# A two-layer transformer block with modulated norms: the last feed-forward, batch by batch, inside the last slots of the attention before it

## Chip, cores and metric

One core of a Trainium2 chip runs the whole program. The time is device microseconds of one execution; the profile is of one such execution. Engines are named as in the profile: PE (TensorE, with PEld for its weight loads), DVE (VectorE), ACT (ScalarE), POOL (GpSimd) and SP (SyncE, here only a queue of transfers). All data are float32 in memory.

## What is computed

Two layers on x of 2 batches, 512 rows and 512 columns. Each is a modulated norm, an attention with a gate, another modulated norm and a feed-forward with a gate. The change concerns the end of layer 1:

```python
h = _layernorm(x) * (1 + ca) + sa
x = x + ga * _L1_attn_ref(h, ...)        # 128 heads, latent 64, head size 4, softmax over 512 keys
h = _layernorm(x) * (1 + cb) + sb
x = x + gb * _L1_ffn_ref(h, ...)

def _L1_ffn_ref(x, base_W, base_b, router_W, router_b, A, B, expert_map):
    base_out = einsum('btd,od->bto', x, base_W) + base_b
    probs = softmax(x @ router_W.T + router_b)          # 15 router outputs
    topk_p, topk_i = top_k(probs, 8)
    w = sum of topk_p over the chosen outputs that expert_map sends to each of 8 experts
    h = einsum('btd,erd->bter', x, A)                   # rank 16 for each expert
    return base_out + einsum('bter,eor->bto', h * w[..., None], B) * 2
```

## The kernel before

Tokens are 8 tiles of 128 rows (`xs[t]`, four for each batch); `hT[b]` holds a batch's normed input turned, features on partitions.

**Layer 1's attention** (`attention1`, from L732) goes over 64 quads: 8 groups of 16 heads (`g`), for each 2 batches, for each 4 quads of 4 heads. For a quad and each of 4 key blocks `i` and two pairs of heads `p`: PE makes scores (`rope`, L948 and L957), ACT copies them out (`keep`, L967), DVE keeps a running maximum (`largest`, L974), transposes it in blocks (`blocks`, L979) and reduces it (`tops`, L985). `twice`, `join` (a PE transposition, `psx`, L997), `top`, `top_hi`, `top_lo`, `stripes` and `row` spread a row's maximum over the keys. It is subtracted on DVE for a quad's first head (`less_even`, L1050) and on POOL for the three others (L1048 and L1054), for two of them from copies that ACT makes (`row_copy`, L1039) and for the third from `row_even` (L1043). ACT takes the exponential (L1057), PE mixes with the values (`mix`, L1103).

The order on the four engines is written out: `PLAN1` (L713 to L729) names for each slot the operations and, by a number, the quad they serve, so that a quad is spread over several slots (`tops 1 -2` is that step for the quad two slots back). `tc.manual_schedule` keeps this order. After a batch's last quad, `leave` (L1111) copies the sum out and puts pieces into two lists: `chain` (`inverse`, `back` and `exact`, `spreading`, `scale` and `both`) and, every second group, `later` (four times `project`, `gated`, `added`), which `extra`, `extra_dve` and `extra_pool` take up in later slots. The loop runs four slots past the last quad, and then empties the lists: the drain. SP's transfers aren't part of the order written out by hand; a scheduler places them.

**The feed-forward** (L393 to L492) has pools of its own and is ordered by the scheduler. Transfers of all its weights and constants come first, the small ones on POOL's queue (L411 to L417). Then for both batches the norm (`Norm.batch`, L205: statistics, root, rows `xn` L184, 16 PE transpositions L193, copies to `hT` with gain and shift, L201 on DVE and L203 on ACT), and on POOL the bias added to x (L428). Then for each batch: 16 router matmuls of 15 columns (`pl`, L434) and 4 that add the router's bias (L441); softmax; for each tile, a rank of every output by five DVE instructions on 15x15 comparisons (L457 to L462: greater, equal, equal times `before`, their sum, a reduction); `psel`, its four transpositions, a matmul to expert weights (`pw`, L472), the low-rank input (`ph`, L475), their product `hw`; and for each tile four matmuls with W (L485), one with the low-rank output (L488), the gate on DVE (L490), x added on POOL (L491) and the output's transfer.

Of the kernel before, what the change touches and what calls it, by code (L numbers as in the profile page):

```python
# [10 lines left out]
F32 = mybir.dt.float32  # L11
# [31 lines left out]
def adaln_kernel(ctx: ExitStack, tc: tile.TileContext, A: dict, out: bass.AP):  # L43
# [19 lines left out]
    ones_row = const.tile([1, P], F32, tag="ones_row", name="ones_row")  # L63
    nc.gpsimd.memset(ones_row, 1.0)
# [81 lines left out]

    def gated_bias(name, gate, pool):

        row = pool.tile([P, D], F32, tag="biasrow", name=f"row_{name}")
        nc.sync.dma_start(out=row, in_=A[name].unsqueeze(0).to_broadcast([P, D]))  # L150
        out = [pool.tile([P, D], F32, tag=f"gb{b}", name=f"gb{b}_{name}") for b in range(B)]
        for b in range(B):
            nc.gpsimd.tensor_mul(out[b], row, gate[b])
        return out
# [134 lines left out]


    with ExitStack() as c01:
# [99 lines left out]
        attention1(tc, A, small, hT, xs, gate[2], ident, normalised, c01.close)  # L391

    with ExitStack() as c3:  # L393
        lnp = c3.enter_context(tc.tile_pool(name="ln", bufs=1))
        fw = c3.enter_context(tc.tile_pool(name="ffn1", bufs=1))
        tmp = c3.enter_context(tc.tile_pool(name="tmp1", bufs=3))
        pmm = c3.enter_context(tc.tile_pool(name="pmm2", bufs=4, space=PSUM))
        gate[5] = gate_tiles(1, 5, fw)
        spread_gates(1, (2, 5), grow[1], pmm, {5: gate[5]})

        wT = fw.tile([P, KC, D], F32, tag="wT", name="wT1")
        nc.sync.dma_start(out=wT, in_=A["L1_ffn_WT"].rearrange("(kc p) o -> p kc o", p=P))
        rT = fw.tile([P, KC, N1], F32, tag="rT", name="rT1")
        nc.sync.dma_start(out=rT, in_=A["L1_ffn_RT"].rearrange("(kc p) n -> p kc n", p=P))
        aT = fw.tile([P, KC, E1 * R], F32, tag="aT", name="aT1")
        nc.sync.dma_start(out=aT, in_=A["L1_ffn_AT"].rearrange("(kc p) e -> p kc e", p=P))
        bT = fw.tile([P, D], F32, tag="bT", name="bT1")
        nc.sync.dma_start(out=bT, in_=A["L1_ffn_BT"])
        gb = gated_bias("L1_ffn_base_b", gate[5], fw)
        rb = fw.tile([1, N1], F32, tag="rb", name="rb1")  # L410
        nc.gpsimd.dma_start(out=rb, in_=A["L1_ffn_router_b"].unsqueeze(0))  # L411
        before = fw.tile([P, N1, N1], F32, tag="before", name="before")
        nc.gpsimd.dma_start(out=before, in_=A["c_before"])
        erow = fw.tile([N1, E1 * R], F32, tag="erow", name="erow")
        nc.gpsimd.dma_start(out=erow, in_=A["c_expert"])
        em_i = fw.tile([N1, 1], I32, tag="em_i", name="em_i")
        nc.gpsimd.dma_start(out=em_i, in_=A["L1_ffn_expert_map"].unsqueeze(1))  # L417
        em = fw.tile([N1, 1], F32, tag="em", name="em")
        nc.vector.tensor_copy(em, em_i)

        route = fw.tile([N1, E1 * R], F32, tag="route", name="route")
        nc.vector.tensor_scalar(route, erow, em, None, ALU.is_equal)

        norm = Norm(1, 3, 4, lnp)
        for b in range(B):
            norm.batch(b, pmm)
            for i in range(TB):
                nc.gpsimd.tensor_add(xs[b * TB + i], xs[b * TB + i], gb[b])  # L428
        for b in range(B):

            pl = pmm.tile([P, TB, N1], F32, tag="mm", name=f"pl{b}")
            for i in range(TB):
                for kc in range(KC):
                    nc.tensor.matmul(  # L434
                        pl[:, i, :],
                        lhsT=hT[b][:, kc, i * P : (i + 1) * P],
                        rhs=rT[:, kc, :],
                        start=(kc == 0),
                        stop=False,
                    )  # L440
                nc.tensor.matmul(pl[:, i, :], lhsT=ones_row, rhs=rb, start=False, stop=True)  # L441
            nm = small.tile([P, TB], F32, tag="nm", name=f"rnm{b}")
            nc.vector.tensor_reduce(nm, pl, AX.X, ALU.max, negate=True)
            pr = tmp.tile([P, TB, N1], F32, tag="pr", name=f"pr{b}")
            nc.vector.tensor_add(pr, pl, nm[:, :].unsqueeze(2).to_broadcast([P, TB, N1]))
            nc.scalar.activation(pr, pr, AF.Exp)
            rs = small.tile([P, TB], F32, tag="rs", name=f"rrs{b}")
            nc.vector.tensor_reduce(rs, pr, AX.X, ALU.add)
            nc.vector.reciprocal(rs, rs)
            nc.vector.tensor_mul(pr, pr, rs[:, :].unsqueeze(2).to_broadcast([P, TB, N1]))  # L450

            rank = tmp.tile([P, TB, N1], F32, tag="rank", name=f"rank{b}")
            for i in range(TB):
                pm = pr[:, i, :].unsqueeze(1).to_broadcast([P, N1, N1])
                pn = pr[:, i, :].unsqueeze(2).to_broadcast([P, N1, N1])
                gt = tmp.tile([P, N1, N1], F32, tag="gt", name=f"gt{b}_{i}")
                nc.vector.tensor_tensor(gt, pm, pn, ALU.is_gt)  # L457
                eq = tmp.tile([P, N1, N1], F32, tag="eq", name=f"eq{b}_{i}")
                nc.vector.tensor_tensor(eq, pm, pn, ALU.is_equal)
                nc.vector.tensor_mul(eq, eq, before)  # L460
                nc.vector.tensor_add(gt, gt, eq)
                nc.vector.tensor_reduce(rank[:, i, :], gt, AX.X, ALU.add)  # L462
            psel = tmp.tile([P, TB, N1], F32, tag="psel", name=f"psel{b}")
            nc.vector.scalar_tensor_tensor(psel, rank, E1 - 0.5, pr, ALU.is_lt, ALU.mult)
            pt = pmm.tile([P, 512], F32, tag="mm", name=f"pselT_ps{b}")
            for i in range(TB):
                nc.tensor.transpose(pt[:N1, i * P : (i + 1) * P], psel[:, i, :], ident)
            pselT = tmp.tile([N1, S], F32, tag="pselT", name=f"pselT{b}")
            nc.scalar.copy(pselT, pt[:N1, :])

            pw = pmm.tile([P, 512], F32, tag="mm", name=f"pw{b}")
            nc.tensor.matmul(pw, lhsT=route, rhs=pselT, start=True, stop=True)  # L472
            ph = pmm.tile([P, 512], F32, tag="mm", name=f"ph{b}")
            for kc in range(KC):
                nc.tensor.matmul(  # L475
                    ph, lhsT=aT[:, kc, :], rhs=hT[b][:, kc, :], start=(kc == 0), stop=(kc == KC - 1)
                )
            hw = tmp.tile([P, S], F32, tag="hw", name=f"hw{b}")
            nc.scalar.mul(hw, ph, 2.0)
            nc.vector.tensor_mul(hw, hw, pw)  # L480
            for i in range(TB):
                t, cols = b * TB + i, bass.ts(i, P)
                ps = pmm.tile([P, 512], F32, tag="mm", name=f"psf1_{t}")
                for kc in range(KC):
                    nc.tensor.matmul(  # L485
                        ps, lhsT=hT[b][:, kc, cols], rhs=wT[:, kc, :], start=(kc == 0), stop=False
                    )
                nc.tensor.matmul(ps, lhsT=hw[:, cols], rhs=bT, start=False, stop=True)  # L488
                y = tmp.tile([P, D], F32, tag="y", name=f"yf1_{t}")
                nc.vector.tensor_mul(y, ps, gate[5][b])  # L490
                nc.gpsimd.tensor_add(y, xs[t], y)  # L491
                nc.sync.dma_start(out=x_out[t * P : (t + 1) * P, :], in_=y)  # L492
# [239 lines left out]
def attention1(tc, A, small, hT, xs, ga, ident, normalised, close):  # L732
# [17 lines left out]
    with ExitStack() as ctx:  # L750
# [109 lines left out]
        chain, later = [], []  # L860
# [250 lines left out]
        def leave(t):  # L1111
# [52 lines left out]
            def gated(i, ps):  # L1164
                y = ap.tile([P, D], F32, tag="y", name=f"y1_{G}_{b}_{i}", bufs=2)
                nc.vector.tensor_mul(y, ps, ga[b])
                return y

            def added(i, y):
                nc.gpsimd.tensor_add(xs[b * TB + i], xs[b * TB + i], y)  # L1170

            chain.append((none, inverse, none))
            chain.append((none, back, exact))
            chain.append((spreading, scale, both if ty else none))
            chain.append(None)
            if ty:
                for i in range(TB):
# [47 lines left out]
        for w in range(2):  # L1225
            spread_up(0, w)
        with tc.manual_schedule(engines=FOUR):
            for t in range(-ahead[0] - 2, NQ - ahead[1]):
                n = t + ahead[0] + 1
                if 0 < n < NQ:  # L1230
                    wqs[n] = load_q(n)
# [5 lines left out]
                for d, f, args in plan:  # L1237
                    if f in ASIDE.values():
                        f(t, *args)
                    elif 0 <= t + d + (2 if f in early else 0) < NQ:  # L1240
                        f(t + d, *args)
# [92 lines left out]
```

## Time and profile before

| | us |
|---|---|
| median of 3 runs | 2544.6 (2543.75 to 2546.12) |
| the profiled execution | 2545.36 |
| its span in the profile | 2543.6 |
| quad 60's transposition `psx` on PE | 2333.2 |
| quad 61's, 62's, 63's | 2354.7, 2374.3, 2397.3 |
| end of the last quad's last `mix` | 2421.6 |
| end of the last projection of the attention | 2435.9 |
| last copies to `hT` of batch 1 end | 2453.0 |
| first `psf` matmul of batch 0, of batch 1 | 2480.6, 2521.1 |
| end of the last addition on POOL | 2540.5 |

Busy in the whole span: PE 2454.6 us, DVE 1672.9, ACT 1400.6, POOL 1592.2. Times in views are from the span's start. A line of the timeline or the chain gives start, duration, engine, line of the kernel and what it writes; "x8" stands for eight instructions that follow each other. A float32 matmul counts as two instructions. "Issue" in the chain is time in which the engine waited for nothing that the profile shows.

### The profile page before, as it was taken

Reading aid. Unit: us, or ns where it says so; the run is one execution under the profiler, and the core shown is the slowest. Engines: PE = TensorE matmul, PEld = TensorE weight load, DVE = VectorE, ACT = ScalarE, POOL = GpSimd, SP = SyncE. Lnnn points to the kernel's source line nnn. Section 1 sums busy time; section 2 is a strip of 40 time slices with the busy share of each in tenths; the row PEclk is TensorE's granted clock in tenths of the full one; section 3 lists DMA queues with packets and bytes.
Section 4 is the critical chain, followed back from the end, with each engine's and each line's share of the span. In section 5 each row is a group of like instructions: output and inputs, shape, how many; then the busy total and the mean of one; then the engine's idle time right before and its main releaser. Section 6 shows DMA issues by size and latency. Waiting matters only on the chain.

```text
span 2543.6 us, 28531 instructions
## 1 busy us (share of the span) xinstructions
PE 2454.6 (97%) x10268; PEld 1148.9 (45%) x10268; DVE 1672.9 (66%) x2323; ACT 1400.6 (55%) x2083; POOL 1592.2 (63%) x1538
## 2 busy tenths in 40 slices
PE   7999999999999999999999999999999999999757
PEld 3555555555555444444444344444444434444233
DVE  4545555555555345788777778777878777887652
ACT  2112212212112215888888788878888878888710
POOL 1333333333333314888888888888888888888841
PEclk9999999999999999999999999999999999999868
DMA  6211101001000101000000000000000000000010
GB/s 233 85 51 64 42 5 38 26 20 38 17 1 7 29 15 33 26 19 24 26 26 26 30 19 25 26 26 26 30 18 26 26 26 25 24 23 17 1 32 33
DMA packets 68477, 81.31 MB, mean 32 GB/s; under 512 B 6865, under 2 KB 49520, under 8 KB 68208
## 3 DMA queue, kind: packets, MB, share of 16 engines
q1 hardware_dynamic: 67984, 79.21, 9.8%
q8 instruction: 81, 1.33, 0.2%
q14 instruction: 60, 0.49, 0.1%
q0 software_dynamic: 352, 0.28, 0.1%
HBM read 77.38 MB, written 2.10 MB: 31 GB/s over the span
## 4 chain that ended last, share of the span: by engine, by line
PE 93%; issue 2%; DVE 2%; POOL 2%; ACT 1%; DMA 0%; SPq 0%; POOLq 0%; DVEq 0%; ACTq 0%
PE s L948 18%; PE psq L881 18%; PE acc L1103 9%; PE ps_q L552 9%; PE pw L664 8%; PE s L957 5%; PE s L603 4%; PE po L650 4%; PE psv L574 2%; PE ps_k L552 2%; PE pt L639 2%; PE psu L900 2%; PE psm L1027 1%; PE psw L1159 1%; PE psf L275 1%
## 5 line engine op out<-in xcount | busy, mean ns | idle before, releaser
L1054 POOL TENSOR_TENSOR ss<-ss,row 128x512 f32<-128x512 f32 x512 | 644.6, 1287 | 39.3 <-ACT row L1039 39.3
L967 ACT COPY ss<-s 128x1024 f32<-128x1024 f32 x512 | 505.6, 1015 | 167.4 <-PE s L957 128.8
L948 PE MATMUL s<-q,ckr 64*128 64x512 f32 x2048 | 552.9, 611 | 7.6 <-ACT ss L967 7.6
L1057 ACT ACTIVATE ss<-ss 128x1024 f32<-128x1024 f32 x512 | 525.7, 1070 | 8.4 <-POOL ss L1048 4.0
L881 PE MATMUL psq<-hT,wqr 128*128 128x512 f32 x1024 | 466.7, 598 | 0.0
L957 PE MATMUL s<-qm,c 64*128 64x512 f32 x1024 | 417.9, 794 | 0.0
L620 ACT ACTIVATE p<-s,nm 128x256 f32<-128x256 f32 (+1 forms) x256 | 111.1, 446 | 488.0 <-DVE nm L616 479.2
L974 DVE TENSOR_TENSOR mx<-s,mx 128x1024 f32<-128x1024 f32 x256 | 306.5, 1218 | 41.1 <-PE s L957 40.1
L562 POOL TENSOR_TENSOR qT<-t_q,t_q 128x512 f32<-128x512 f32 x64 | 81.3, 1270 | 402.4 <-DVE t_q L561 402.4
L1048 POOL TENSOR_TENSOR ss<-ss,rowe 128x512 f32<-128x512 f32 x256 | 323.3, 1286 | 0.0
L881 PEld LDWEIGHTS psq<-hT,wqr 128*128 128x128 f32 x1024 | 189.0, 189 | 242.3 <-issue 211.7
L948 PEld LDWEIGHTS s<-q,ckr 64*128 64x128 f32 x2048 | 183.4, 186 | 212.7 <-ACT ss L967 97.2
L1103 PE MATMUL acc<-ss,vp 128*32 128x512 f32 x2048 | 265.7, 607 | 5.5 <-ACT ss L1057 5.5
L974 DVE TENSOR_TENSOR mx<-s,ss 128x1024 f32<-128x1024 f32 x128 | 156.8, 1225 | 117.5 <-ACT row L1039 78.0
L664 PE MATMUL pw<-wo,oT 128*128 128x512 f32 x512 | 230.3, 592 | 0.0
L552 PE MATMUL ps_q<-hT,wq 128*128 128x512 f32 x512 | 230.1, 592 | 0.0
L979 DVE STREAM_TRANSPOSE mx<-mx 128x1024 f32<-128x1024 f32 x128 | 158.6, 1239 | 2.2
L985 DVE TENSOR_REDUCE m<-mx 128x32 f32<-128x1024 f32 x128 | 156.2, 1220 | 4.4
L1050 DVE TENSOR_TENSOR ss<-ss,psm 128x512 f32<-128x512 f32 x256 | 158.0, 679 | 0.0
L957 PEld LDWEIGHTS s<-qm,c 64*128 64x128 f32 x1024 | 104.2, 187 | 117.7 <-issue 114.8
L1017 POOL TENSOR_TENSOR st<-mh,own_block 128x512 fp32r<-128x512 f32 x64 | 67.1, 1048 | 139.0 <-DVE mh L1013 139.0
L552 PEld LDWEIGHTS ps_q<-hT,wq 128*128 128x128 f32 x512 | 96.0, 190 | 102.4 <-issue 100.8
(193 smaller groups left out, 3089.3 us busy)
## 6 DMA issues: line engine op xcount, KB each, us to landing
wqr<-in_L_attn_Wq_rope_pairs SPq DMA_DIRECT2D x64, 512.0 KB
wmod<-in_L_wmod SPq DMA_DIRECT2D x12, 1024.0 KB
wq<-in_L_attn_wq SPq DMA_DIRECT2D x8, 1024.0 KB
wo<-in_L_attn_wo SPq DMA_DIRECT2D x8, 1024.0 KB
x<-in_L_attn_x SPq DMA_DIRECT2D x8, 256.0 KB
wk<-in_L_attn_wk SPq DMA_DIRECT2D x8, 256.0 KB
wv<-in_L_attn_wv SPq DMA_DIRECT2D x8, 256.0 KB
wT<-in_L_ffn_WT SPq DMA_DIRECT2D x2, 1024.0 KB
```

The source lines that it names most:

```text
L552: nc.tensor.matmul(ps, lhsT=wcols(kc), rhs=hT[b][:, kc, :], start=(kc == 0), stop=(kc == KC - 1))
L664: nc.tensor.matmul(ps, lhsT=oTs[u][:, hh, i * P : (i + 1) * P], rhs=groups[g]["o"][:, hh, :], start=(hh == 0), stop=(hh == GRP - 1),)
L881: nc.tensor.matmul(ps, lhsT=wqs[t][:, kc, pair * P : (pair + 1) * P], rhs=hT[b][:, kc, :], start=(kc == 0), stop=(kc == KC - 1),)
L948: nc.tensor.matmul(out[:, j, :], lhsT=whole[b]["kr"][r, bass.ts(i, P)], rhs=qs[t, p][r, :], start=True, stop=False,)
L957: nc.tensor.matmul(out[:, j, :], lhsT=qkc[t // 2, 1][r, bass.ts(i, P)], rhs=qm[t, p][r, :], start=False, stop=True,)
L967: nc.scalar.copy(ss[t, i, p], hold["s", t, i, p])
L974: nc.vector.tensor_max(mx[t, p], hold["s", t, i, p], before)
L979: nc.vector.transpose(m, m)
L1048: nc.gpsimd.tensor_sub(s, s, hold["r", t, 2])
L1054: nc.gpsimd.tensor_sub(s, s, hold["r", t, 2 * p + 1])
L1057: nc.scalar.activation(ss[t, i, p], ss[t, i, p], AF.Exp)
L1103: nc.tensor.matmul(accs[g, b][32 * h : 32 * (h + 1), :], lhsT=vps[t][:, kb, h, :], rhs=ss[t, kb, h // 2][:, h % 2, :], start=(s == 0 and k ...
```

## The change

The separate feed-forward, its pools and `gated_bias` are gone. A class `Ffn1` holds its steps, on tiles that the attention's pools already have (by tag: constants on `clq0`, the gates and low-rank weights on `q0` and `q1`, rows on `mx0`, `mx1` and `s`, results of `base` on the scores' two-bank tiles `s0` and `s1`, the rest on `pX`). `attention1` gets this class as `ffn` and issues it all by hand:

- W's two halves are loaded behind the last query weights, into their tiles (tag `wq`); all constants go on SP's queue.
- The loop over slots ends three slots earlier. A table `beside` puts work behind named operations of slots 62 to 64: group 7's batch 0 from `inverse` to its four projections (two of the four sums on DVE instead of POOL), constants, `routes`, gates, batch 0's statistics, root and first rows.
- `tail` writes out the rest: the end of quad 63 with batch 0's last rows, turn and router logits among it; then batch 0's feed-forward, the attention's output for batch 1, batch 1's norm, and its feed-forward.
- In quad 63, DVE subtracts the maxima of both first heads straight from PSUM, and in the two last key blocks one more head's; `row_even` falls away there.
- The router's bias is added on DVE with the copy out of PSUM, in place of a matmul.
- Ranks: one comparison (greater or equal) for all four tiles of a batch, times `before`; the rank is its sum along one axis, less its sum along the other, plus 14 - m. 900 elements an instruction, in place of five instructions of 225 for each tile. Two steps of `tail` run a small `ready` activation, by which ACT loads the table of the next function early.

```diff
+    class Ffn1:
...
+        def rows(self, t):
+            b, i = divmod(t, TB)
+            if i % 2 == 0:
+                tag, n = (f"mx{i // 2}", 1) if b == 0 else ("s", 16)
...
+        def chosen(self, b):
...
+            nc.vector.tensor_tensor(
+                w,
+                pr.unsqueeze(2).to_broadcast(full),
+                pr.unsqueeze(3).to_broadcast(full),
+                ALU.is_ge,
+            )
+            before = self.before[:, :N1, :].unsqueeze(1).to_broadcast(full)
+            nc.vector.tensor_mul(v, w, before)
+            nc.vector.tensor_reduce(self.r1, v, AX.X, ALU.add)
+            nc.vector.tensor_reduce(self.r2, v.rearrange("p t n m -> p t m n"), AX.X, ALU.add)
+            nc.vector.tensor_sub(self.r1, self.r1, self.r2)
...
+        def base(self, t):
+            b, i = divmod(t, TB)
+            if i % 2 == 0:
+                self.ps[b, i // 2] = self.pS.tile(
+                    [P, 2, D], F32, tag=f"s{i // 2}", name=f"psf1_{t}"
+                )
...
+        def leave(self, t, pool):
+            b, i = divmod(t, TB)
+            y = self.ap.tile([P, 2, D], F32, tag="s", name=f"yf1_{t}", bufs=16)[:, 0, :]
+            nc.vector.tensor_mul(y, self.ps[b, i // 2][:, i % 2, :], self.gate[b])
+            (nc.gpsimd if pool else nc.vector).tensor_add(y, xs[t], y)
+            nc.sync.dma_start(out=x_out[t * P : (t + 1) * P, :], in_=y)
...
+        beside = {
+            (Z - 1, "leave"): [lambda: last[0](0), F.constants],
+            (Z - 1, "blocks 1"): [turned_back],
+            (Z, "rope 0 1"): [scaled],
+            (Z, "mix 3"): [do(projected, 0), do(projected, 1)],
+            (Z, "rope 3 1"): [do(projected, 2), do(projected, 3), last.clear],
+            (Z + 1, "keep 0 1"): [F.routes],
+            (Z + 1, "row 0"): [do(F.gates, 0)],
+            (Z + 1, "largest 1 0"): [do(F.stats, 0), do(F.stats, 1)],
+            (Z + 1, "largest 2 0"): [do(F.stats, 2), do(F.stats, 3)],
+            (Z + 1, "mix 3"): [do(F.gates, 1)],
+            (Z + 1, "exponential 0 0"): [do(F.scale, 0)],
+            (Z + 1, "tops 0"): [do(F.rows, 0), do(F.rows, 1)],
+            (Z + 1, "mix 0"): [do(own_values, Z)],
+        }
...
+        def part(i, odd):
+
+            for p in range(2):
+                less(Z, p, i, 0, nc.vector)
+                less(Z, p, i, 1, nc.vector if p and odd else nc.gpsimd)
+                exponential(Z, p, i)
+
+        def tail():
...
+            mix(Z - 1, 3)
+            part(0, False)
+            for kc in range(2):
+                F.turn(0, kc)
+            part(1, False)
+            mix(Z, 0)
+            for kc in range(2, KC):
+                F.turn(0, kc)
+            part(2, True)
+            mix(Z, 1)
+            F.logits(0)
+            part(3, True)
+            mix(Z, 2)
+            F.probs(0)
+            mix(Z, 3)
+            leave(Z)
+            F.ready(AF.Sqrt)
+            last[0](0)
+            last[1](0)
+            last[2](0)
+            F.base(0)
+            F.base(1)
+            scaled()
+            F.chosen(0)
+            F.bias(0)
+            F.hidden(0)
+            projected(0)
+            projected(1)
+            F.stats(TB)
...
+            F.scale(1)
+            F.ready(AF.Exp)
+            F.base(2)
+            for t in range(TB, NT):
+                F.rows(t)
+            F.weighed(0)
+            for t in range(TB):
+                F.add_bias(t)
+            F.turn(1, 0)
+            F.turn(1, 1)
+            F.low(0)
+            F.low(1)
+            F.turn(1, 2)
+            F.turn(1, 3)
+            F.logits(1)
+            F.probs(1)
+            F.leave(0, True)
+            F.leave(1, True)
+            F.base(3)
+            F.low(2)
+            F.low(3)
+            F.chosen(1)
+            F.hidden(1)
+            F.leave(2, True)
+            F.leave(3, True)
+            F.bias(1)
...
+            F.base(TB)
+            F.base(TB + 1)
+            F.weighed(1)
+            for i in range(2):
+                F.low(TB + i)
+                F.leave(TB + i, i == 0)
+            F.base(TB + 2)
+            F.low(TB + 2)
+            F.leave(TB + 2, True)
+            F.base(TB + 3)
+            F.low(TB + 3)
+            F.leave(TB + 3, False)
```

## The prediction

> **What bounds the kernel now.** I read the page's slices first, to see where the time is not filled, then the busy time by stretch, then the chain that ended last, then single groups in the timeline.
>
> The page's slices, 63.6 us each (PE TensorE, DVE VectorE, ACT ScalarE, POOL GpSimd; busy tenths; PEclk granted clock):
>
> ```profile
> PE   7999999999999999999999999999999999999757
> DVE  4545555555555345788777778777878777887652
> ACT  2112212212112215888888788878888878888710
> POOL 1333333333333314888888888888888888888841
> PEclk9999999999999999999999999999999999999868
> ```
>
> The reader sees a full PE up to slice 37; only the last three slices have room, and only they are touched by the change. Next those slices as stretches, cut at my landmarks: last transposition that both kernels reach with the same order (2333.2), end of the last quad's last mix (2421.6), end of the last projection (2435.9), end of the second norm (2452.2), then batch 0's routing, its matmuls, and the same for batch 1.
>
> ```profile
> core 0: us, PE busy (x) PEld busy (x) DVE busy (x) ACT busy (x) POOL busy (x), PEclk, DMA share, GB/s
> 2333.20:2359.90 26.70, 26.70 (x134) 11.06 (x135) 20.48 (x30) 21.94 (x28) 21.55 (x24) 1.00 0.01 2
> 2359.90:2421.60 61.70, 46.42 (x209) 14.00 (x205) 38.90 (x50) 41.49 (x47) 54.67 (x52) 0.86 0.00 0
> 2421.60:2435.90 14.30, 7.53 (x12) 3.24 (x13) 7.85 (x18) 3.24 (x5) 7.45 (x10) 0.64 0.44 139
> 2435.90:2452.20 16.30, 6.52 (x33) 4.61 (x32) 14.23 (x22) 3.30 (x5) 16.17 (x12) 0.68 0.00 1
> 2452.20:2471.10 18.90, 9.10 (x40) 8.76 (x41) 8.29 (x27) 1.54 (x2) 0.00 (x0) 0.50 0.00 0
> 2471.10:2497.70 26.60, 25.94 (x54) 10.99 (x55) 2.77 (x4) 1.17 (x2) 3.80 (x3) 0.84 0.08 30
> 2497.70:2511.10 13.40, 5.30 (x42) 4.97 (x41) 8.18 (x27) 0.25 (x1) 1.27 (x1) 0.71 0.05 20
> ```
>
> To 2359.9 PE is full. In the drain of the attention (61.7 us) POOL is busy 54.7 us: it is the bound there. From 2421.6 to the end, 122.0 us, one engine works while three wait: projection, norm, routing on DVE, matmuls, batch 0, then the same for batch 1. The chain shows it in single pieces (start, us, engine and line):
>
> ```profile
> 2443.96 5.76 DVE xn L184 x4
> ...
> 2461.30 9.79 issue
> 2471.08 1.02 PE pselT_ps L467 x4
> 2472.11 0.02 issue
> 2472.13 0.58 ACT pselT L469
> 2472.72 0.04 issue
> 2472.76 2.07 PE pw L472 x2
> 2474.83 5.91 PE ph L475 x8
> ```
>
> PE waits 9.8 us for 25 small DVE instructions, then runs `ph` at half clock (5.91 us; its equal `psf` takes 3.43 at full clock). So the resource is idle time of PE in a serial tail. The change puts batch 0's norm, turn and logits before 2421.6 and overlaps batch 1's attention output and routing with batch 0's matmuls.
>
> **The drain, to the last mix.** The instructions as built stand in the same order up to quad 61's transposition, but for a few places at the start (loads of the first 100 us; I give that ±1 us). On SyncE's queue the bias and constant loads now stand ahead of the last four query loads. The first of them waits until batch 0's query parts (tag `chq0`) are read for the last time, in `inner` for quads 58 and 59, two slots early; a query load is issued 32.8 us before its first use (2311.6 to 2344.4 for the last), so a delay below that costs nothing. The weights follow those loads, the outputs come last. POOL loses four DMA issues (0.52 to 0.60 each), which lie around 2430 in a wait for the projection: nothing.
> 1. Quad 61's transposition. The inverse of group 7's batch 0 now stands ahead of the last two DVE transposes and reduces: 0.70+0.55+0.24+0.28, and the turn back 0.70, with gaps and waits **+3.5**. Before, DVE did these in holes.
> 2. To quad 62's. `scale` (0.75) and the POOL `both` it starts (1.28) stand ahead of quad 61's top values: 2.0. Four projections stand inside quad 62's scores: PE 4×0.86=3.4, 1.7 of it at half clock, so 5; DVE 0.69 of a multiplication and two adds of 0.69. An add beside POOL is bounded by `xn` (below): 0 to 0.95 of wait each; I take half, 1. All together **+11**, from 5 (half in holes of ACT and PE) to 13.
> 3. To quad 63's. Two table loads on ACT (1.28 each), square root 0.30, two rows `xn`, the aggregates; statistics and gates were there before. **+4**, bounds +2 and +6.
> 4. To the last mix. POOL's last-quad subtractions fall from 12 to 6: -7.5 (1.245 apart); the `rowe` copy, -0.6. DVE gets six more: 6×0.60=3.6. Added ahead of the last mix: two `xn`, 16 transposes (0.14 each at full, 0.24 at half clock) 3, two ACT copies of 0.78 between exponentials, two DVE copies of 0.81, and 16 logits matmuls, 3.8 at full clock (2497.74: 0.96 for four) and 7.3 at half (2452: 1.82). Sum 3.6+2+3+1.6+1.6+6=17.8, less 8.1, less about 6 that runs while PE waits for exponentials: **+3.5**, bounds 0 and +9.
>
> Sum +22: the last mix ends at **2443.6**, bounds 2432 and 2453.
>
> The costliest unknown is the small DVE work beside a busy POOL. Two timeline rows (start, us, engine, instruction) bound it:
>
> ```profile
> 2438.21 0.98 DVE L184 TENSOR_SCALAR xn<-x,mv,rstd 128x512 f32<-128x512 f32 x2
> 2443.96 5.75 DVE L184 TENSOR_SCALAR xn<-x,mv,rstd 128x512 f32<-128x512 f32 x4
> ```
>
> 0.49 each, against 1.44 each while POOL runs its chain of adds (L428, from 2441.51). I use 0.49 to 1.44, middle 0.97. For additions of two SBUF tiles on DVE the trace has no wide row beside a busy POOL; I give them the same bounds.
>
> The Trainium skill (SBUF — State Buffer, Who interferes with whom) speaks against the change here: a VectorE instruction with two SBUF inputs, or in a two-port mode, and a GpSimd instruction that reads SBUF block each other wholly. It would let every such DVE instruction wait up to a POOL instruction of 1.29 us; for the eight wide ones (four adds, two subtractions, two rank steps) that is, as an estimate, 5 us later, 2531 instead of 2526.
>
> **From the last mix to the end.** Followed along the built order:
> 1. `base` 0 and 1: 8×0.86=6.9, 0.9 more at half clock: 7.8. It hides the last group's copy, table load and inverse (0.60+1.28+0.70+0.55+0.24+0.28+0.71+0.61=5.0).
> 2. Spread 0.45, scale 0.75: 1.2.
> 3. Ranks of batch 0. L459 takes 0.386 for 225 elements and L450 0.22 for 60, so 1.0 ns an element: one instruction of 900 costs 1.06. Four of them and six of about 0.21, 5.6; with gaps and waits for POOL's two instructions 8.0 (5.6 to 10).
> 4. Batch 1's four multiplications 0.60 apart, two adds with half waits, statistics 4×0.85: 2.4+2.4+3.4=8.2.
> 5. Root 0.30, reciprocal 0.17, rows 4×0.97: 4.4. ACT's two table loads lie under step 4 and the rows.
> 6. Four turns of 4 transposes, `low` 0 and 1, last copy 0.81: 2.6+2.6+0.9=6.1.
> 7. Logits 3.8.
> 8. `base` 3, `low` 2 and 3, `ph`, `base` 4 and 5: 18×0.86=15.4, 1 more at half clock: 16.4. It hides batch 1's ranks (before, PE waited 8.1 us for them at 2503).
> 9. Four transposes 0.7, copy 0.57, `pw` 0.86, product 0.69: 2.9.
> 10. `low` 4, its multiplication, `low` 5 (same two-bank tile, so it waits for that read): 0.86+0.69+0.86, 1.2 at half clock: 3.6.
> 11. `base` 6 and `low`, multiplication, `base` 7 and `low`, multiplication, DVE add: 4.3+0.69+4.3+0.69+0.69, 1.2 at half clock: 11.9. Nothing hides this.
> 12. Output transfer: 3.1 (2540.5 to 2543.6).
>
> Sum 77.4; with some 40 handovers between engines at 0.04 to 0.1, 3.5 more, **81**, against 122 now. Bounds 68 (full clock, no waits) and 92 (upper ends, 6 more of half clock). Span 2443.6+81=2524.6. The profiled execution took 2545.36 with a span of 2543.6; the median of the runs is 2544.6, 1.0 over the span. So I predict **2526 us**.
>
> Table loads: in the trace one starts at 2428.89, 0.02 after the copy ahead of it, and its user 1.30 later; I price 1.28. The skill (ScalarE: Activation LUTs, What ACT_TABLE_LOAD costs) adds a drain and says about 2.66; by it the two in the drain would cost 2.8 more, 2529.
>
> **Rivals.**
> - A: DVE becomes the drain's bound. Each small DVE instruction waits nearly a whole POOL one; drain +28, and with ranks and rows at their upper ends a tail of 85: 2421.6+28+85+1.0, that is 2536 (2533 to 2541). For: in the drain POOL runs its subtractions back to back. Against: it has six fewer at the end.
> - B: the inserted work falls into holes. DVE idles 22.8 of 61.7 us in the drain, ACT 20.2. Drain +14, tail 76: 2421.6+14+76+1.0, that is 2513 (2506 to 2518). Against: it stands in front of the few instructions that quads 62 and 63 hang on.
> - C, slower: PE's clock stays at half from the last mix on. The path has some 42 us of matmuls at full clock, and the sum holds 5 more for half clock; all at half adds 37: 2563. It decides from 24 us on (2549.7 is 0.2% over 2544.6), so when some 70% of that PE work runs at half. For: 0.50 throughout 2452 to 2471, when PE ran 15-column matmuls. Against: in both dense stretches the clock came back after some 7 us.
> - D: nothing gained, 2544: a tile's release holds the new work until the attention is through. The built waits show no such cycle, only the two-bank ones in steps 10 and 11.
>
> **Numbers.** Forecast 2518 to 2533: 0.62; A 0.15; B 0.15; C 0.05; D 0.03. What a measurement of this kernel can tell from no change is about 0.2%, 5 us. Faster takes the forecast, B and 0.14 of A: 0.91; within 0.2% the rest of A and D: 0.04; slower C: 0.05. The range 2515 to 2538 leaves 0.11 above (C, D, the end of A) and 0.07 below (half of B).
>
> **What would show it.** Last mix near 2444, quad 62's transposition some 14 us later than 2374.3; PE idle before `pselT` of batch 1 under 2 us; the tail after the last mix near 81 us; last output 3.1 us behind a DVE add. Wrong if the last mix comes before 2432 or after 2453, if wide DVE adds take over 1.5 us, or if the clock stays at 0.5 past the `base` of batch 0.

## The result, and the profile after

The changed kernel takes 2519.6 us (median of 4 runs, 2519.35 to 2523.97), a ratio of 0.9906 to the kernel before, interval 0.9891 to 0.9921: 0.9% faster. (One run of the kernel before took 3641 us and is left out.) The profiled execution took 2519.66 with a span of 2517.9. The page's slices, 62.9 us each:

```profile
PE   8999999999999899999999999999999999999877
DVE  4445555555555435787778777778778877788764
...
POOL 1333333333334323888888888888888888888643
PEclk9999999999999999999999999999999999999978
```

PE's last three slices went from 7, 5, 7 to 8, 7, 7; POOL's from 8, 4, 1 to 6, 4, 3. The stretches of the changed kernel, cut at the transpositions `psx` of quads 60, 61, 62 and 63, the last mix, and three marks in the tail (length, then busy time of PE, PEld, DVE, ACT and POOL, each with its count, granted clock, DMA share, GB/s):

```profile
2329.74:2353.89 24.15, 22.09 (x105) 8.64 (x103) 19.49 (x26) 19.35 (x24) 18.26 (x19) 1.00 0.09 24
2353.89:2384.90 31.01, 22.00 (x95) 7.74 (x95) 22.52 (x27) 17.25 (x20) 22.17 (x21) 0.89 0.05 16
2384.90:2410.65 25.75, 19.01 (x83) 6.62 (x84) 20.98 (x32) 19.88 (x24) 17.64 (x21) 0.85 0.06 21
2410.65:2438.77 28.12, 23.98 (x110) 11.61 (x110) 11.98 (x21) 12.01 (x15) 9.89 (x8) 0.62 0.00 1
2438.77:2447.00 8.23, 8.23 (x19) 3.81 (x19) 2.48 (x5) 2.07 (x3) 0.61 (x1) 0.89 0.00 0
2447.00:2466.43 19.43, 12.66 (x28) 5.05 (x26) 18.54 (x28) 2.84 (x5) 9.55 (x8) 0.91 0.00 0
2466.43:2494.30 27.87, 27.69 (x90) 14.83 (x91) 14.82 (x23) 2.40 (x4) 10.07 (x9) 0.88 0.10 38
2494.30:2517.90 23.60, 15.82 (x31) 5.98 (x29) 4.84 (x7) 0.57 (x1) 4.58 (x4) 0.81 0.12 45
```

The reader sees: the stage before the last mix (28.12) has no full engine, POOL is busy 9.89 of it, and PE runs at a clock of 0.62; from 2447.0 to 2466.4 DVE is the bound (18.54 of 19.43); then PE is (27.69 of 27.87), with batch 1's ranks hidden beside it. The tail as a whole, from the last mix to the end: of the kernel before, of the changed one, and of a run told below that has batch 0's norm, turn and logits in the tail too (e4_tail):

```profile
2421.58:2543.60 122.02, 81.01 (x230) 43.58 (x229) 44.79 (x102) 10.68 (x17) 33.76 (x29) 0.72 0.10 34
2438.78:2517.90 79.12, 64.39 (x165) 29.66 (x165) 40.68 (x62) 7.89 (x13) 24.81 (x20) 0.87 0.07 27
2418.51:2509.20 90.69, 72.58 (x218) 37.37 (x217) 44.97 (x72) 13.57 (x20) 25.02 (x20) 0.87 0.06 24
```

PE was idle for 41.0 us of the tail before and is for 14.7 now; its work there is 16.6 shorter: part of it now stands ahead of the last mix, and the granted clock is 0.87 instead of 0.72.

All kernels below are compared by stages of their profiled executions, because executions of one kernel differ by some us ahead of quad 60 (last section). A stage runs from one `psx` to the next (quad 60's starts at 2333.0 in the kernel before, not at 2333.2); "mix" from quad 63's to the last mix; tail from there to the end; "sum" from quad 60's on. Stages with the same instructions differ by up to 1.6 between profiles (29.4 and 31.0, 25.8 and 27.1), so a smaller difference is not read.

| kernel | 61 | 62 | 63 | mix | tail | sum | median |
|---|---|---|---|---|---|---|---|
| before | 21.7 | 19.6 | 23.0 | 24.2 | 122.0 | 210.5 | 2544.6 |
| **after** | 24.2 | 31.0 | 25.8 | 28.1 | 79.1 | 188.2 | 2519.6 |
| e1_memset | 21.7 | 19.6 | 21.9 | 24.2 | 121.8 | 209.1 | 2541.1 |
| e2_ranks | 24.1 | 29.4 | 27.1 | 27.4 | 80.3 | 188.2 | 2519.3 |
| e3_share | 24.1 | 30.8 | 27.1 | 21.4 | 80.2 | 183.6 | 2515.1 |
| e4_tail | 24.1 | 29.4 | 22.5 | 15.8 | 90.7 | 182.4 | 2511.0 |
| e5_pool | 24.1 | 27.4 | 26.5 | 28.1 | 82.4 | 188.5 | 2519.9 |
| e7_lows | 24.1 | 31.0 | 25.8 | 28.1 | 77.1 | 186.1 | 2519.5 |
| e8_psb | 24.1 | 30.8 | 27.0 | 27.4 | 74.6 | 183.9 | 2515.9 |
| e9_banks | 24.1 | 31.0 | 25.8 | 28.3 | 78.9 | 188.1 | 2519.6 |
| e10_best | 24.2 | 25.8 | 22.6 | 16.5 | 75.2 | 164.2 | 2495.7 |
| e11_out | 24.1 | 22.5 | 22.5 | 15.8 | 100.1 | 185.0 | 2521.6 |
| e12_gates | 24.2 | 25.8 | 22.6 | 16.5 | 74.3 | 163.4 | 2496.8 |
| e13_warm | 24.1 | 31.0 | 25.8 | 25.1 | 78.8 | 184.7 | 2517.4 |

So the change lost 20.5 in the drain (109.0 against 88.6), won 42.9 in the tail, and quad 60 came 3.3 earlier: together 25.7 between the two profiles.

### The profile page after: what moved, and what is told of

The parts are those of the page before. It is cut to its first block, busy times and chain, and to the rows that moved or that the text cites. A ratio compares the mean times of both kernels' runs of the same rounds, so it can differ in the third digit from the quotient of the medians.

```text
span 2517.9 us, 28439 instructions
## 1 busy us (share of the span) xinstructions
PE 2453.7 (97%) x10252; PEld 1146.2 (46%) x10252; DVE 1684.2 (67%) x2309; ACT 1401.9 (56%) x2086; POOL 1571.9 (62%) x1521
## 4 chain that ended last, share of the span: by engine, by line
PE 95%; DVE 3%; ACT 1%; DMA 0%; issue 0%; POOL 0%; SPq 0%; DVEq 0%; ACTq 0%; POOLq 0%
PE s L1081 19%; PE psq L1014 18%; PE acc L1236 10%; PE ps_q L685 9%; PE pw L797 8%; PE s L1090 5%; PE s L736 4%; PE po L783 4%; PE psv L707 2%; PE ps_k L685 2%; PE pt L772 2%; PE psu L1033 2%; PE psm L1160 2%; PE psw L1292 1%; PE psf L499 1%; PE psf L264 1%
## 5 line engine op out<-in xcount | busy, mean ns | idle before, releaser
L1187 POOL TENSOR_TENSOR ss<-ss,row 128x512 f32<-128x512 f32 x504 | 634.5, 1287 | 42.8 <-ACT row L1172 42.8
L1181 POOL TENSOR_TENSOR ss<-ss,rowe 128x512 f32<-128x512 f32 x252 | 317.9, 1285 | 0.0
```

The source lines that it names most:

```text
L1181: nc.gpsimd.tensor_sub(s, s, hold["r", t, 2])
L1187: nc.gpsimd.tensor_sub(s, s, hold["r", t, 2 * p + 1])
```

## Experiments

**The 3.3 us ahead of quad 60** (e1_memset, the kernel before with one line moved).

```diff
-    nc.gpsimd.memset(ones_row, 1.0)      # at the start
+        nc.gpsimd.memset(ones_row, 1.0)  # in the feed-forward
```

> The kernel before with one edit: the memset of ones_row (0.20 us on POOL at 0.91) stands at the start of the feed-forward instead of the program's start. Theory: the whole 3.3 us by which quad 60's transposition came earlier in the changed kernel is this memset's place. The coefficient load stands right behind it on POOL (issued at 1.50 before, 1.31 after), and the schedule as built then puts the first coefficients' three small DVE steps ahead of the row statistics instead of behind four of them. PE's first matmul at about 7.8 instead of 13.3, quad 60's transposition at 2329.9 instead of 2333.2, time 2541.3. Rival: the 3.3 us come from something else of the change (loads, tiles); then PE's first matmul stays near 13.3 and the time at 2544.6.

Measured: 2541.1 against 2544.2 beside it, ratio 0.9986 (0.9976 to 0.9995). The timeline of the kernel before, and of this one, at the start:

```profile
13.34 6.11 PE L103 MATMUL psr<-wmod,sc 128*32 128x512 f32 x16 [13.34 <-DVE sc L88]
```

```profile
7.63 2.39 PE L101 MATMUL psr<-wmod,sc 128*32 128x512 f32 x3 [7.63 <-DVE sc L86]
```

PE starts 5.7 us earlier; some 3 of them last (by the interval, 1.3 to 6.1). The theory holds: a memset of 0.2 us stood ahead of a load (issued at 1.50, now at 1.31), and the scheduler answered with another order on DVE. The profile's quad 60 came 1.2 earlier only (2331.8), with a clock of 0.87 instead of 0.91 from 20 to 60 us; e7_lows and e12_gates, below, which hold the change and have 0.87 there too, reach it at 2331.1 and 2331.7. Up to there PE and ACT now run in the changed kernel's order, so nothing is left to the rival on these two engines.

**The ranks** (e2_ranks): for each tile

```diff
-            nc.vector.tensor_tensor(w, pr..., pr..., ALU.is_ge)   # 900 elements, and 5 more
+            for i in range(TB):   # is_gt, is_equal, mul, add, reduce: 225 elements each
```

> The changed kernel with the ranks of each tile by the five instructions of before (greater, equal, equal times before, sum, reduction; 225 elements each). Theory: on batch 0 the ranks stand on the path (2447.7 to 2455.9, 8.2 us, of which the six rank steps are 6.4 by the rows 2.07, 1.10, 1.09, 1.66, 0.22, 0.22); 20 instructions at 0.39 and 0.02 to 0.1 between them are 8.0 to 9.8, so +1.6 to +3.4; on batch 1 they lie beside 16 us of matmuls and cost nothing. Time 2521 to 2523. Rival: the one comparison carries much of the gain, with both batches on the path: +8 or more, 2528.

Measured: sum 188.2 as in the changed kernel, tail +1.2, 2519.3, where the theory had 2521 to 2523. The ranks of batch 0 took 10.4 (2442.84 to 2453.21) instead of 8.2. The one comparison is worth 1 to 2 us in the tail, nothing that the times show.

**Shared subtractions** (e3_share): `less_even` and `less_odd` for the last quad (three of four heads on POOL), `row_even` back.

```diff
-                less(Z, p, i, 0, nc.vector)
-                less(Z, p, i, 1, nc.vector if p and odd else nc.gpsimd)
+                less_even(Z, p, i)
+                less_odd(Z, p, i)
```

> The changed kernel with the last quad's subtractions divided as before: POOL takes three of four heads in every key block, with the row_even copy back on ACT. Theory by the prediction's step 4: POOL's 6 more subtractions at 1.245 and the copy 0.6 are 8.1 later, DVE's six fewer 3.6 earlier, so the last mix comes 4.5 us later, up to 8 (2443 to 2447), time 2524 to 2528. Rival: in the changed kernel PE sets this stage (24.0 of 28.15 us busy, granted clock 0.62), POOL is busy 9.9 of it and has room for 7.5 more; then the last mix moves by 0 to 1.5 and the time stays at 2519.6 to 2521.

Theory and rival both failed: the stage got 6.7 **shorter** (21.4), 2515.1. In the changed kernel this happens in the stage (timeline):

```profile
2425.18 0.76 ACT L406 ACTIVATE hT<-pst,mod,mod 128x512 f32<-128x512 f32 x1
2425.99 0.66 PE L397 MATMUL pst<-ident,xn 128*128 128x128 f32 x4 [2.68 <-ACT hT L406]
...
2426.69 0.81 DVE L404 TENSOR_SCALAR hT<-pst,mod,mod 128x512 f32<-128x512 f32 x1 [2.91 <-PE pst L397]
2427.41 1.27 DVE L1402 TENSOR_TENSOR ss<-ss,psm 128x512 f32<-128x512 f32 x2
2428.19 7.01 PE L412 MATMUL pl<-ffnc,hT 128*128 128x15 f32 x32
2428.21 4.07 ACT L1190 ACTIVATE ss<-ss 128x1024 f32<-128x1024 f32 x4 [2.27 <-DVE ss L1402]
```

A circle of in-order queues: ACT copies one turned block, PE waits 2.68 for that copy, DVE waits 2.91 for PE's next block, and DVE's subtractions, now six more, stand behind; ACT's exponentials wait 2.27 for them. Then PE runs the router matmuls for 7.01. With most subtractions on POOL the circle is open, and the same matmuls take 3.75 (e3_share):

```profile
2427.36 3.75 PE L412 MATMUL pl<-ffnc,hT 128*128 128x15 f32 x32
```

The 6.7 come in three parts: counted from `psx`, the router matmuls start 2.8 earlier, they run 3.3 shorter at a granted clock of 1.00 instead of 0.50, and the last mixes behind them take 2.98 instead of 3.64. So 4.0 of it go with the clock; e13_warm, below, wins 3.1 of the stage with the subtractions left on DVE.

**Batch 0's work out of the drain** (e4_tail):

```diff
-            (Z + 1, "exponential 0 0"): [do(F.scale, 0)],
-            (Z + 1, "tops 0"): [do(F.rows, 0), do(F.rows, 1)],   # gates, statistics, turn, logits, softmax too
+            leave(Z)   # then all of it, in the tail; behind it the spread, then base 0 and 1
```

> The changed kernel without batch 0's work in the drain: its gates, statistics, root, rows, turn, router logits and softmax are issued after the last mix, ahead of the last group's inverse and spread, instead of within slots 62 to 64; batch 0 of group 7's attention output stays in the drain, and the tail's overlap of the two batches stays. Theory: the drain gets back 2.7 (quad 62 to 63) and about 8 of the last stage (28.15 back to about 20), so the last mix comes about 2428; behind it statistics 3.4, root and rows 3 to 4.5, turn 3, logits 4 to 7, softmax 1.3 stand on the path, 15 to 19, less what lies beside the last group's inverse (about 2.5). Net +2 to +6, 2522 to 2526. Rival 1: the place in the drain carries the gain: the drain gives back only the 2.7 and the tail grows by the full 19, 2536. Rival 2: it is worth nothing, or less: 2517 to 2520.

Measured: 2511.0; drain 17.3 shorter, tail 11.5 longer, sum -5.7: rival 2, and more than it said. But the edit does a second thing: the last group's spread, which stood behind base 0 and 1, now stands ahead of both. The run e8_psb, below, moves it ahead of base 1 alone, with batch 0's work left in the drain, and that is worth 4.2 in the sum (183.9). Against e8_psb the drain is 17.6 shorter, the tail 16.1 longer and the sum 1.5 lower, within the 1.6 by which equal stages differ. So the runs show that the place in the drain, as built, gains nothing; that it loses isn't shown, and with the subtractions back on POOL as in e3_share (4.5 in the sum) and the spread as in e8_psb it might gain, which wasn't run. Here the shared subtractions do pay: the stage takes 15.8 against 24.2 before.

**Additions on POOL** (e5_pool): `last[8](i, y)` without the engine.

> The changed kernel with all eight additions of the last projection on POOL, instead of every second on DVE. An addition takes 0.69 alone on DVE (2502.33), 1.01 to 1.27 beside POOL, and 1.27 on POOL. Theory: beside a POOL addition the one on DVE takes as long as on POOL, so the pair saves little: the second addition of a pair ends 1.27 behind the first instead of 0.6, statistics wait for it, twice in the tail: +1.3, and in the drain 0 to 1: 2520 to 2522. Rival by the rule that two-input DVE instructions and POOL block each other: taking four of them off DVE frees more than it costs, 2517.

2519.9: stage 62 shorter by 2.0 to 3.6 (that stage's own spread is 1.6), tail longer by 3.2. Split additions pay in the tail, where POOL has room, and cost about as much in the drain, where it is busy.

**Four places of the tail and the last stage.** e7_lows puts the four low-rank matmuls behind all bases, e8_psb the spread ahead of base 1, e9_banks the turn on the scores' tiles, e13_warm three idle matmuls into PE's hole:

```diff
-            F.base(1)
             scaled()
+            F.base(1)                                        # e8_psb
```

```diff
+            for _ in range(3):                               # e13_warm, ahead of the last turn
+                nc.tensor.matmul(warm[:, 0, :], lhsT=ident, rhs=F.wT[0][:, 0, :], start=True, stop=True)
```

> The changed kernel with base 6 and 7 ahead of batch 1's expert weights, then the four low-rank matmuls together, then the four multiplications. Theory by the prediction's steps 10 and 11 (low 5 waits for the multiplication of tile 4 in the same two-bank tile, and nothing hides base 6 and 7): three waits of 0.78 and PE at half clock go, the expert weights come 6.9 later, and behind them stand 4 low-rank matmuls (3.4 to 6.9), one multiplication, one addition, the output: 2504.4 + 3.4 + 0.7 + 0.7 + 3.2 + handovers is a span of 2512.6, time 2514.4, to 2517 at half clock. Rival: no gain, 2519.6, since base 6 and 7 then stand on the path in place of the waits.

2519.5, no gain by the times; tail -2.0 of the theory's 5.2 (2.6 at half clock). The four matmuls took 5.40, between the theory's 3.4 and 6.9, and the additions beside POOL's took 1.28 each.

> The changed kernel with the last group's spread (psb) and scale ahead of base 1 instead of behind it. Theory: from 2447 to 2467 DVE is the bound of the tail (17.8 of 18.7 us busy, PE idle 3.56 and 3.21), and its queue starts with the scale, which waits for psb behind base 1 on PE although the inverse is ready at 2442.83, 3.3 us earlier. So scale, ranks, projection and norm come 3.0 earlier, base 1 fills PE's idle time: 2516.6. Rival: the time goes into a longer wait further on (PE has 3.4 more to do before the second batch's turn), 2519.

2515.9, tail -4.5, more than the 3.0: the spread now waits 0.49 for the inverse instead of behind base 1.

> The changed kernel with one edit: the four turned blocks of batch 0 go to the two two-bank tiles of the scores (free since the last key block was copied), instead of the pool of three single banks, of which the last quad's two rows of maxima hold two until DVE's last subtraction. Theory: in the changed kernel one free bank chains the turns (each transposition waits until the copy of the one before has left, 0.87 and 2.68 idle on PE), DVE's subtractions stand behind its copies, and the exponentials wait for them (2.25 and 2.27 on ACT). With four banks the stage from quad 63's transposition to the last mix shrinks from 28.1 by about 4.5, to 23.6, near the 21.4 that it takes with the subtractions on POOL; time 2515. Rival: the 32 router matmuls at half clock (7.0 us) ahead of the last two mixes set the stage; then it shrinks by 1 at most, 2518.5.

2519.6, nothing. It didn't test its theory: both blocks of a pair lie in one two-bank tile, and PE's waits stayed (0.87 and 2.75). Banks remain untested; the hole itself is what e13_warm takes.

> The changed kernel with three more matmuls of 128x512 on PE (identity by a weight tile, a product that nobody reads, 0.86 each at full clock) ahead of batch 0's last turned block, where PE waits 2.68 us for a copy on ACT. Nothing else is changed; the output stays the reference's. Theory: the stage from quad 63's transposition to the last mix is long because of PE's clock, not because of the work put in: the granted clock is 1.00 from 2420 to 2426, PE then has this hole, and the clock is 0.5 from 2427 to 2441; the 32 router matmuls take 7.01 (3.75 in the run with the subtractions on POOL, where the hole is 0.63), the last 16 mixes 3.64 (2.98). With the hole filled the clock stays full: the last mix 3.3 to 4 earlier, base 0 and 1 up to 0.8 shorter, 2515 to 2516 in spite of 2.6 us more work. Rival: the clock falls for another reason (what PE does, or the earlier holes); then the last mix moves by 0 to +0.5 and the time stays at 2519.6 to 2520.

2517.4 (ratio 0.9894, 0.9877 to 0.9910), 1.4 more than the theory's upper end; the last mix comes 3.1 earlier with 2.6 us **more** work on PE. Clock around the hole, of the changed kernel and of this one (the number before the last two in a line):

```profile
2424.00:2426.00 2.00, 0.01 (x1) 0.01 (x1) 0.00 (x0) 1.94 (x3) 0.00 (x0) 1.00 0.00 0
2426.00:2428.00 2.00, 2.00 (x12) 0.57 (x12) 1.31 (x2) 0.00 (x0) 0.00 (x0) 0.72 0.00 0
2428.00:2430.00 2.00, 2.00 (x13) 1.81 (x9) 2.00 (x5) 1.73 (x2) 0.00 (x0) 0.50 0.00 0
2430.00:2436.00 6.00, 6.00 (x31) 5.31 (x34) 1.72 (x5) 2.28 (x3) 0.00 (x0) 0.50 0.01 3
```

```profile
2424.00:2426.00 2.00, 1.90 (x7) 0.68 (x6) 0.00 (x0) 1.65 (x3) 0.00 (x0) 1.00 0.00 0
2426.00:2428.00 2.00, 2.00 (x19) 0.99 (x17) 1.60 (x3) 0.08 (x1) 0.00 (x0) 1.00 0.00 0
2428.00:2430.00 2.00, 2.00 (x21) 2.00 (x20) 2.00 (x4) 1.94 (x3) 0.00 (x0) 1.00 0.03 8
2430.00:2436.00 6.00, 6.00 (x27) 2.85 (x27) 1.46 (x5) 2.67 (x5) 0.00 (x0) 0.50 0.00 0
```

The clock stays full 3 us longer and is at half for 6.8 us (2430.0 to 2436.8) instead of 13.6 (2426.9 to 2440.5); the router matmuls take 4.56. It still falls from 2430 on, without a hole just ahead, and that fall isn't explained. A candidate is the router matmuls themselves, 15 columns wide, which run there (2427.29 to 2431.85): in the changed kernel's tail the clock falls at 2478.1 with no hole ahead, right behind batch 1's (2473.12 to 2477.26), and in e12_gates at 2452.8, within them (2450.30 to 2455.01). But in e3_share it stays at 1.00 through them. No run takes them away.

**The projections out of the drain too** (e11_out, from e4_tail): `projected` for group 7's batch 0 behind the last mix.

> The run without batch 0's work in the drain, with one thing more taken out of the drain: group 7's batch 0 keeps its inverse and scale there, but its four projections, multiplications and additions are issued after the last mix, ahead of batch 0's statistics. Theory: steps 1 and 2 of the prediction (12 to 14 us by which quads 61 and 62 come later) are mostly these projections in front of quad 62's top values; the stages to quad 61's and 62's transposition shrink from 24.1 and 29.4 towards 21.7 and 19.6 (the inverse stays, so 24 and 22), the last mix comes 7 to 9 earlier; behind it eight multiplications and additions, 8.2 by the same steps on batch 1, stand on the path, all but 1 to 2: net -1 to +2, 2510 to 2513. Rival: the projections lie in holes of the drain and cost 3 or less there: +5, 2516.

Stage 62 -6.9, as the theory had it, but tail +9.4: sum +2.5 against e4_tail. The profiled execution took 2513.2; the three others 2521.2 to 2522.0, and no profile tells why.

**A new order** (e10_best), and one edit of it (e12_gates):

```diff
+            scaled()                    # e10_best, in the middle of base 0
+            for i in range(2):          # batch 1: projection, statistics; scale, rows
...
+            F.chosen(0)                 # then batch 0's ranks
```

> A new order of the same work, from what the runs so far showed. Drain: batch 0's statistics stay there (in a hole of 3.98 us that DVE has in the run without batch 0's work), its root, table loads and rows go into the hole after quad 63's transposition (ACT 3.73, DVE 2.43), its turn behind the last subtractions, router logits and gates behind the last mix; the additions of group 7's batch 0 go to POOL. Tail: spread and scale in the middle of base 0, batch 1's projection and norm ahead of batch 0's ranks on DVE, copies of batch 1's turn on ACT, low-rank matmuls of batch 1 behind two bases, tile 7 on a two-bank tile of its own. Theory (the drain is worth most when its last quads are left alone, and the tail is bound by PE, with about 60 us of matmuls, if DVE's chain of batch 1 goes first): from quad 60's transposition 90 to the last mix, as in the run without batch 0's work (91.8) less 2 to 3 for the additions, then a tail of 70 to 74: 2327 to 2331 + 162 + 1.7, that is 2491 to 2495. Rival: DVE stays the bound of the tail whatever its order (50 us of instructions, a third of them up to twice as long beside POOL): a tail of 80 to 84, 2501 to 2505.

2495.7, ratio 0.9809 (0.9793 to 0.9825): faster than both kernels. Last mix at 89.0 behind quad 60, as expected; tail 75.2, 1.2 over the theory's upper end. Of the 23.9 that the sum gains on the changed kernel, 20.0 lie ahead of the last mix and 3.9 behind it, although part of batch 0's turn, its logits and gates now stand in the tail. It isn't the order alone: two additions go to POOL, copies of the turn to ACT, and tile 7 gets a two-bank tile of its own; these were not run one by one. From the last mix to 2476:

```profile
2416.03:2476.00 59.97, 56.87 (x186) 29.82 (x187) 31.69 (x57) 11.46 (x18) 22.13 (x18) 0.89 0.05 18
```

PE is busy 56.87 of 59.97, DVE 31.69: the tail is PE's now.

> The new order with one edit: the two gates and batch 0's bias work stand behind base 2 instead of between batch 1's projection and batch 0's router logits. Theory: the tail is bound by PE (57 of 60 us busy from 2416 to 2476), so what is left to gain is PE's waits and its half clock: between 2426.4 and 2439 the granted clock is 0.73, behind 0.68 of wait for a gate's copy, and router logits, base 1 take 5.3 and 5.4 instead of 3.8 and 3.6; the rows beside POOL's bias additions take 2.88 instead of 2.16. Without the gates there: 2 to 4 less, 2492 to 2494. Rival: the clock drops by the waits for batch 1's multiplications all the same: 0 to 1 less, 2495.

2496.8 (ratio 0.9811), tail -0.9: the rival's size, but not its mechanism. Base 1 and the router matmuls ran at full clock (3.68 and 3.64), but the two gates (2.0) and half clock (32 to 42 us behind the last mix, from within batch 1's router matmuls) came back further on.

## Why the prediction was right, point by point

The forecast was 2526; the 6.4 us that it was too high are 3.3 at the start, 1.5 in the drain (+20.5 for +22) and 1.9 in the tail (79.1 for 81), less 0.3 between span and time. The mechanism, PE's idle time in the serial tail, is what the runs show; that the drain came out within 1.5 is partly luck (step 4). Of the signs named, the last mix came at 2438.8 for 2444, quad 62's transposition 13.9 later for 14 (counted from quad 60's), and PE didn't wait before batch 1's `pselT`.

- **The start, "±1 us"**: missed by 2.3. The instructions' places were seen, their effect on DVE's queue wasn't priced (e1_memset).
- **Step 1**: +2.5 for +3.5. **Step 2**: +11.4 for +11; e11_out shows 6.9 of it in the projections, e5_pool 2.0 to 3.6 in the two additions on DVE.
- **Step 3**: +2.7 for +4. The tables cost 1.28 to 1.30 each: for the tail's load at 2464.42, shown below, the user starts at 2465.72. The Trainium skill (ScalarE: Activation LUTs, What ACT_TABLE_LOAD costs) adds a drain of 1.38, which no row here shows.
- **Step 4**: +3.9 for +3.5, right by luck: two errors of 4 cancel. For the subtractions its terms give -4.5 (-7.5, -0.6 and +3.6); with no work of batch 0 in the stage they are worth -8.5 (e4_tail, 15.8 for 24.2). For the work added its terms give 8.2 (14.2, less the 6 beside PE's waits); it cost 12.4 (28.1 for 15.8). And with the turn in the queues POOL is no longer the stage's bound: giving the subtractions back to POOL makes it shorter (e3_share). The 6 for the logits were 7.0, at half clock.
- **Tail, items 1 to 5**: 8.0 for 7.8 to the spread; ranks 8.2 for 8.0; projection to statistics 8.2 for 8.2; root to rows 4.5 for 4.4. The rows of the changed kernel's timeline show what POOL adds to DVE:

```profile
2449.05 1.27 POOL L354 TENSOR_TENSOR gb<-biasrow,g 128x512 f32<-128x512 f32 x1
2449.21 2.07 DVE L451 TENSOR_TENSOR rank<-rank 128x900 f32<-128x900 f32 x1
...
2457.11 1.26 DVE L1303 TENSOR_TENSOR x<-x,y 128x512 f32<-128x512 f32 x1
```

In e10_best, where POOL rests, the same comparison is:

```profile
2439.01 1.09 DVE L457 TENSOR_TENSOR rank<-rank 128x900 f32<-128x900 f32 x1
```

The 2.07 reads as a wait until POOL's addition ends (2450.32) and then 0.96; the addition ends 0.55 behind POOL's at 2456.55 (1.27), and takes 0.69 alone. The Trainium skill (SBUF — State Buffer, Who interferes with whom) says that the two block each other wholly; the rows agree but for some 0.13. Its +5 didn't come on top: the four additions waited 0.32 to 0.58 and batch 0's comparison 0.98, which the half waits of the drain's step 2 and of the tail's items 3 and 4 had about priced, while the subtractions waited for nothing (0.69) and batch 1's comparison is hidden.
- **"ACT's two table loads lie under step 4 and the rows"**: not quite. The second stood ahead of the copy of `pselT`, and PE waited 3.21 for that copy, 1.28 of it the load:

```profile
2464.42 1.28 ACT L376 ACT_TABLE_LOAD   x1
...
2465.82 0.56 ACT L487 COPY pselT<-pselT_ps 15x512 f32<-15x512 f32 x1
...
2466.43 1.12 PE L489 MATMUL pw<-pselT,route 15*128 15x512 f32 x2 [3.21 <-ACT pselT L487]
```

- **Items 6 and 7**: 8.6 for 9.9. **Items 8 and 9**: 17.1 and 3.2 for 16.4 and 2.9, batch 1's ranks hidden without a wait on PE. **Items 10 and 11**: 17.1 for 15.5, three waits of 0.78 and `low` and base 6 at half clock. **Item 12**: 3.2 for 3.1, behind the DVE addition at 2513.96.
- **Rivals**: A's mechanism is real (1.26 for 0.69), its size isn't: the DVE additions cost 2.0 to 3.6 in the drain. B and D didn't come. C's clock was back to full by 2442, though half clock is part of what made the last stage long (3.1 by e13_warm).

Most of the tail's 42.9 doesn't need the drain: with none of batch 0's norm, turn and logits there it is still 31.3 (e4_tail), 22.9 of it PE's idle time (41.0 before, 18.1 in that run). It comes from the tail as it is written out, with one batch's work beside the other's; the ranks are 1.2 of it (e2_ranks), and the other pieces were not taken apart. The placement of this part inside the attention's last slots, the change's own idea, gains nothing as built: 17.3 lost in the drain for 11.5 in the tail, or for 16.1 with the spread placed as in e8_psb. That of the projections wins 2.5 in the one profiled execution of e11_out; its three others are 8 us longer.

## What to carry to other kernels

Put work into a hole only if nothing in the in-order queues behind it is waited for by an engine on the path: here a turn through PE, ACT and DVE in the middle of an exponential's queue, with the rows and logits around it, cost the drain at least what it saved behind it. Price a stage's PE work by the clock that its holes will leave. And try another order of the whole end, drain and tail, before splitting instructions: a new order with a few changes of engine was worth another 24 us here, 20 of them ahead of the last mix.

## What the runs showed that was not expected

- A hole of 2.7 us on PE was followed, within 2 us, by a clock of 0.5 from 2427 to 2440. The Trainium skill (TensorE: Matmul & The Clock Gate, HAM oscillation — how this bites in real kernels) gives the rule as "no PE-idle gaps >~3.4µs"; here a shorter one was followed by half clock, and filling it kept the clock for 3 us. In e10_best holes of 2.16 and 2.53 us (from 2390.89 and 2397.01) were followed by 0.5 as well.
- From 20 to 60 us PE is idle for 2.2 to 2.9 us in all, 2.11 of it in one hole at about 46 to 49. In four of the fourteen profiled executions (e2, e4, e10, e11) the clock then stayed at 1.00; in the others it was 0.5 for 6.8 or 10.2 us from about 50 on. In the thirteen kernels in which PE runs the same order up to quad 60 (all but the kernel before) this sorts the time of quad 60: 2326.5 to 2327.0 with the full clock, 2329.5 to 2330.6 after 6.8 us of half clock, 2331.1 to 2331.8 after 10.2. So a median of four runs can hide or feign 3 us.
- The reduction along the strided axis (L460) takes 1.66 where the one along the dense axis (L459) takes 1.09, with POOL at rest.
